# A 256-column first weight slice and six idle matmuls in the opening of a fused attention and 4-bit feed-forward kernel

## The chip, the cores and the metric

The kernel runs on one core of a Trainium2 chip. A core has five engines that run side by side, each with its own instruction stream: TensorE (PE in the profile, its weight loads PEld), VectorE (DVE), ScalarE (ACT), GpSimd (POOL) and SyncE (SP), which here only issues transfers. They meet at semaphores. The metric is device time of one execution in microseconds (us), lower is better. The profile is of one execution of its own.

## The reference

Everything is float32, with x and ctx of shape (32, 64, 512). The core of what is computed:

```python
x = x + xattn(layernorm(x), ctx, ctx, Wq, bq, Wk, bk, Wv, bv, Wo, bo)
x = x + ffn(layernorm(x), gate_w, gate_z, gate_s, up_w, up_z, up_s, down_w, down_z, down_s)

# xattn: 8 heads of 64 columns; W* are 64x64 and act on the axis of length 64
q, k, v = (einsum('oi,bil->bol', W, x) + b[:, None] for each of the three)
p = softmax(q_h @ k_h.T / sqrt(64))
out = einsum('oi,bil->bol', Wo, heads(p @ v_h)) + bo[:, None]

# ffn: integers 0..15, a zero and a scale for each group of 128 rows and each column
W = (w - repeat(z, 128, axis=0)) * repeat(s, 128, axis=0)
out = (silu(x @ W_gate) * (x @ W_up)) @ W_down       # 512 -> 1792 -> 512
```

## The kernel before

**Tiling.** Two batch entries make a *pair* of 128 rows, so there are 16 pairs; four pairs make a *block* of 512 token columns, and there are four blocks. The attention of block 0 has nothing to hide behind. The attention of blocks 1 to 3 is spread over the rounds of the feed-forward (FFN) of the block before it.

**The opening.** The string `START` (L741) is an order written out by hand. Each word such as `2.turn` is a method of `Attention` for one pair: `stats` and `scale` and `apply` (layer norm; `scale` is the power on POOL, L381, and `apply` L112), `k`, `q`, `scores`, `v`, `turn` (softmax weights times Wo, L497), `weigh` (L513), `residual` (L525, which also stores the new x, L528), then `stats2`, `scale2`, `apply2` for the second layer norm, `flip` (transposes on PE, L536) and `high` and `low` (L546 on ACT and L550 on DVE). The last two split the transposed activations into two halves, `hTh` and `hTl`, whose sum is the float32 value. `x_out` words finish a step on ACT or DVE. The opening runs under `tc.manual_schedule()`, so each engine gets its instructions exactly in this order. After it a scheduler orders each engine's stream.

**Weights.** The 4-bit integers come from DRAM as int32 into `ng`, `nu` (gate and up, four row groups `g` of 128 rows, 1792 columns) and `nd` (down, 14 groups of rows). They are loaded by POOL's DMA queue (`load_wide`, `load_down`) in the column slices of the list `wide`: 512, 512, 512, 256 columns. Then the zero point is subtracted in place: POOL does it for each (group, gate or up) piece of a slice (L302), DVE for each row of `nd` (L308). One such subtraction is one step of the generator `weight_steps`; the word `integers` in `START` takes one step. The zero points have first been cast and written to DRAM (`zeros_to_dram`, the word `zeros`), and `load_zeros` reads them back broadcast to 128 partitions, on SP's queue, into `z16` (bfloat16, for gate and up) and `z8` (for down). The pool `zeros` has one buffer of each, so the next slice's zeros are loaded when the last piece of the slice before has been computed.

**The FFN loop.** `gate_up(t, f)` (L595) works on 128 of the 1792 hidden columns: for each of four row groups it does two matmuls of `pg` and two of `pu` (L604), and ACT scales the sum between groups (L614). The last group ends in the Silu (L617), the product `h` on DVE (L620), and its split into `hh` and `hl` on POOL (L630, L631). Two lanes, even and odd f, run two rounds apart; `down(t, f)` (L636) follows six rounds behind. A round (L864) advances the lanes, the attention of the next block, the downs, and `weights`. In round 0, 5 and 13 `load_weights` issues the loads of slices 1, 2 and 3. The first matmul at L604 needs `hTh` of all four pairs, and its PSUM bank is one that the opening's transposes used, so the last `low` must have read it.

**Waiting for products.** `behind_products` makes the first instruction after it wait for the last PE instruction written so far, so that a transfer starts no earlier than that.

Of the kernel before, what the change touches and what calls it, by code (L numbers as in the profile page):

```python
# [26 lines left out]
def kernel(  # L27
# [41 lines left out]
    nc = tc.nc  # L69
# [44 lines left out]
    with ExitStack() as fast:  # L114
# [17 lines left out]

        PARTS = ("c", "xn", "k_eT", "q_e", "v")

        def places(pool):
# [25 lines left out]
        bqk = bias[:, : 2 * D].rearrange("p (m d) -> p m d", m=2)  # L163
        bvo = bias[:, 2 * D :]
        CW = 512
        wide = [(c, min(CW, I - c)) for c in range(0, I, CW)]
        w_T = const.tile([P, 4, D], F32, tag="w_T", name="w_T")
        WK, WV, WQ, WO = range(4)

# [95 lines left out]
        def load_wide(w: bass.AP, src: bass.AP, at: int, n: int):  # L265

            newest["POOL"] = nc.gpsimd.dma_start(w[:, :, at : at + n], src[:, :, at : at + n]).ins

        def load_down(at: int, n: int):
            fs = slice(at // P, (at + n) // P)  # L270
            newest["POOL"] = nc.gpsimd.dma_start(nd[:, fs, :], down_rows[:, fs, :]).ins

        def load_weights(at: int, n: int):

            load_wide(ng, gate_rows, at, n)
            load_wide(nu, up_rows, at, n)
            load_down(at, n)

        def load_zeros(at: int, n: int):
            z16 = zeros.tile([P, 2, KT, CW], BF16, tag="z16", name=f"z16_{at}")  # L280
            z8 = zeros.tile([P, KT, CW], U8, tag="z8", name=f"z8_{at}")
            for m in range(2):
                nc.sync.dma_start(
                    z16[:, m, :, :n], z_rows[m, :, at : at + n].partition_broadcast(P)
                )
            nf = n // P
            zd = z8_dram[at // P * L : (at // P + nf) * L]
            nc.sync.dma_start(
                z8[:, :nf, :].rearrange("p f l -> p (f l)"), zd.partition_broadcast(P)
            )  # L290
            return z16, z8

        def weight_steps(zs):

            for i, (at, n) in enumerate(wide):
                if i:
                    zs = load_zeros(at, n)
                z16, z8 = zs
                for g in range(KT):
                    for m, dst in enumerate((ng, nu)):  # L300
                        piece = dst[:, g, at : at + n]
                        nc.gpsimd.tensor_tensor(  # L302
                            piece, piece.bitcast(F32), z16[:, m, g, :n], ALU.subtract
                        )
                        yield
                for i in range(n // P):
                    piece = nd[:, at // P + i, :]
                    nc.vector.tensor_tensor(piece, piece.bitcast(F32), z8[:, i, :], ALU.subtract)  # L308
                    yield
# [19 lines left out]
        class Attention:  # L329
# [201 lines left out]
            def flip(self):  # L531
                two = self.tile("ph")[:, : self.n, :]
                self.ph = two.rearrange("p i (c d) -> p c i d", d=P)
                for i in range(self.n):
                    for c in range(KT):
                        nc.tensor.transpose(  # L536
                            self.ph[:, c, i, :], self.at["xn"][:, i, ts(c, P)], ident
                        )

            def columns(self, h: dict):  # L540
                t, i = divmod(self.p, PB)
                cols = h[t][:, :, i * P : (i + self.n) * P]
                return cols.rearrange("p c (i d) -> p c i d", d=P)
# [190 lines left out]
        def chain(*gens):  # L734
# [6 lines left out]
        START = """  # L741
            0.stats 0.scale 0.apply 1.stats projections 1.scale biases
            projections_out 1.apply 2.stats 0.k biases_out 2.scale 3.stats 0.q 1.q
            0.k_out 3.scale 0.q_out 1.k gate zeros 1.q_out 0.scores 1.k_out 2.k
            3.apply 1.scores broadcast 0.highest 2.apply 2.k_out 0.less 0.v
            1.highest 0.exp 2.q 1.less 0.v_out 3.q 0.sums 1.exp 2.v 2.q_out 0.divide
            3.k up 2.v_out 1.sums 2.scores 3.q_out 1.divide 3.k_out 1.v 2.highest
            3.scores 1.v_out 2.less 1.turn 3.highest 2.exp 0.turn rows 3.less
            1.turn_out 2.sums 3.exp 1.weigh 0.turn_out 3.sums 2.divide 3.v
            1.residual 1.stats2 3.divide 0.weigh 3.v_out 2.turn 0.residual 0.stats2  # L750
            1.scale2 3.turn down 2.turn_out 2.weigh 3.turn_out 1.apply2 0.scale2
            scales 2.residual 2.stats2 3.weigh scales_out 1.flip 3.residual 3.stats2
            2.scale2 1.high 0.apply2 3.scale2 integers integers integers integers
            2.apply2 0.flip 1.low 2.flip 3.apply2 0.high quotients 3.flip 2.high
            0.low 3.high 2.low 3.low
        """
        place = places(att)
        with (
            tc.tile_pool(name="early", bufs=1) as early,
            tc.tile_pool(name="att0", bufs=1) as att0,  # L760
            tc.tile_pool(name="ps0", bufs=4, space=bass.MemoryType.PSUM) as ps0,
            tc.manual_schedule(),
        ):
            w_nat, b_nat = projection_loads()
# [12 lines left out]
            def first_banks(name: str):  # L777
                return ps0.tile([P, 2, CW], F32, tag="s", name=name)

            @contextmanager  # L780
            def behind_products():

                traced = nc.cur_bb.bb.instructions
                last = next(i for i in reversed(traced) if i.engine == mybir.EngineType.PE)
                n = len(traced)
                yield
                first = traced[n]
                tc.add_manual_dep(  # L790
                    first,
                    last.name,
                    mybir.DependencyInfo(
                        mybir.DependencyClass.Sync, mybir.DependencyReason.DATA
                    ),
                    reason="behind products",
                )

            pairs = [Attention(p, 1, at_first[p // SET], first_banks) for p in range(PB)]
            halves = {}  # L800
            for step in START.split():
                if step[0].isdigit():
                    getattr(pairs[int(step[0])], step[2:])()
                elif step == "gate":
                    load_wide(ng, gate_rows, *wide[0])
                elif step == "zeros":
                    zeros_to_dram()
                elif step == "broadcast":
                    with behind_products():
                        weights = weight_steps(load_zeros(*wide[0]))  # L810
                elif step == "up":
                    with behind_products():
                        load_wide(nu, up_rows, *wide[0])
                elif step == "rows":
                    with behind_products():
                        load_rows(PB // SET)
                elif step == "down":
                    with behind_products():
                        load_down(*wide[0])
                elif step == "integers":  # L820
                    next(weights)
                elif step == "quotients":
                    quotients()
                elif step.endswith("_out"):
                    next(halves[step[:-4]], None)
                else:
                    halves[step] = {
                        "projections": lambda: projections(w_nat),
                        "biases": lambda: biases(b_nat),
                        "scales": lambda: scales(s_nat),  # L830
                    }[step]()
                    next(halves[step])
# [30 lines left out]
        with ExitStack():  # L863
            for r in range(NBLK * ROUNDS + LAG):  # L864
# [16 lines left out]
                with ExitStack() as behind:  # L881
                    for ins in newest.values():
                        behind.enter_context(tc.issue_after(ins))
                    if r in (0, 5, 13):
                        load_weights(*wide[(0, 5, 13).index(r) + 1])
                    if r < ROUNDS:
                        advance(weights, 2 if r < 4 else 1 + r % 2)
                    else:
                        advance(tops, 1 + (r % 4 == 3))
                    if k in FINISH_AT or k + 2 in FINISH_AT:  # L890
                        advance(finishing)
# [120 lines left out]
```

## Time and profile before

| | |
|---|---|
| median of three runs | 457.89 us (454.89 to 458.46) |
| the profiled execution's own time | 457.63 us |
| its span in the profile | 455.3 us |
| busy: PE, PEld, DVE, ACT, POOL | 413.0, 315.3, 330.5, 309.3, 280.4 us |
| matmuls of the FFN, L604 gate and up, mean | 398 to 407 ns, 224 of each of four kinds |
| gate and up integers, L302, mean | 1060 and 1072 ns, 16 of each |
| loads of 1 MB, issue to landing (gate, up, down) | 5.9, 7.9 and 9.6 us |

The span is the time from the first to the last instruction that the profile shows; the 2.3 us between it and the execution's own time lie around it. A busy PE isn't PE at its peak, since the ends of matmuls are modelled. Busy shares are averages: the opening, up to the first L604 at 43.85 us, has another limit than the loop.

### The profile page before, as it was taken

The numbers are of one execution on the slowest core, as the hardware profiler recorded it, in microseconds if no ns is written. First come the engines' busy times: TensorE is split into PE (matmuls) and PEld (weight loads), VectorE is DVE, ScalarE is ACT, GpSimd is POOL, SyncE is SP. The second block draws the span as 40 slices with busy tenths as digits, with TensorE's granted clock in tenths as the row PEclk, the third lists the DMA queues.
The fourth block names the chain that finished last, engine by engine and source line by source line (L and its number), as shares of the span: only waits on it lengthen the run. The fifth ranks groups of instructions, "written<-read, shape, count | busy, mean of one in ns | idle before, by whom it ended". The sixth has DMA issues, their size and how long they took to land.

```text
span 455.3 us, 10322 instructions
## 1 busy us (share of the span) xinstructions
PE 413.0 (91%) x4175; PEld 315.3 (69%) x4175; DVE 330.5 (73%) x510; ACT 309.3 (68%) x473; POOL 280.4 (62%) x293
## 2 busy tenths in 40 slices
PE   4854998998999999999999899999999999999991
PEld 4642564766677776777778577786778888887870
DVE  5959553797979983696869775586869655668672
ACT  2332489665787669686788569785688788777750
POOL 5335749658474487676787676664566887883311
PEclk9988799999999999999999999999999999999996
DMA  6677959436102020141000012130001012100004
GB/s 205 204 246 229 254 188 273 118 100 183 53 26 74 2 93 1 45 141 50 1 23 25 2 48 94 48 94 1 1 1 48 1 47 94 46 1 0 1 2 145
DMA packets 20928, 36.55 MB, mean 80 GB/s; under 512 B 1848, under 2 KB 7432, under 8 KB 20872
## 3 DMA queue, kind: packets, MB, share of 16 engines
q1 hardware_dynamic: 14056, 24.20, 16.2%
q0 software_dynamic: 6208, 11.01, 8.8%
q8 instruction: 35, 0.57, 0.5%
q10 hardware_dynamic: 608, 0.59, 0.4%
q14 instruction: 21, 0.17, 0.1%
HBM read 27.37 MB, written 8.42 MB: 79 GB/s over the span
## 4 chain that ended last, share of the span: by engine, by line
PE 45%; POOL 23%; issue 15%; DVE 10%; ACT 4%; DMA 1%; ACTq 0%; POOLq 0%; DVEq 0%
PE pg L604 11%; PE pu L604 11%; PE pd L649 6%; POOL hl L631 6%; PE pd L652 5%; POOL squares L325 4%; POOL squares L323 4%; POOL hh L630 3%; DVE xn_set L112 2%; DVE y L660 2%; POOL nu L302 2%; POOL q_e_set L488 1%; POOL ng L302 1%; DVE k_eT_set L411 1%; DMA w_nat<-in_L_xattn_Wo_dram 1%
## 5 line engine op out<-in xcount | busy, mean ns | idle before, releaser
L660 DVE SCALAR_TENSOR_TENSOR y<-pd,s_all,y 128x512 f32<-128x512 f32 x204 | 150.1, 743 | 47.6 <-PE pd L652 45.1
L614 ACT ACTIVATE pg<-pg,s_q 128x512 f32<-128x512 f32 x168 | 111.5, 665 | 76.4 <-PE pg L604 75.0
L614 ACT ACTIVATE pu<-pu,s_q 128x512 f32<-128x512 f32 x168 | 110.7, 659 | 4.5 <-PE pu L604 4.4
L604 PE MATMUL pg<-hTh,ng 128*128 128x512 f32 x224 | 91.3, 407 | 6.3 <-POOL nu L302 2.9
L649 PE MATMUL pd<-hh,nd 128*128 128x512 f32 x224 | 93.9, 419 | 1.6 <-DVE y L660 1.1
L630 POOL CAST hh<-h 128x512 fp32r<-128x512 f32 x55 | 35.0, 636 | 93.0 <-DVE h L620 91.2
L604 PE MATMUL pu<-hTh,nu 128*128 128x512 f32 x224 | 90.6, 404 | 0.9 <-POOL nu L302 0.5
L604 PE MATMUL pu<-hTl,nu 128*128 128x512 f32 x224 | 89.3, 399 | 0.0
L604 PE MATMUL pg<-hTl,ng 128*128 128x512 f32 x224 | 89.2, 398 | 0.0
L652 PE MATMUL pd<-hl,nd 128*128 128x512 f32 x224 | 88.7, 397 | 0.0
L631 POOL TENSOR_TENSOR hl<-h,hh 128x512 fp32r<-128x512 f32 x55 | 72.0, 1310 | 4.4
L620 DVE SCALAR_TENSOR_TENSOR h<-pu,s_all,g 128x512 f32<-128x512 f32 x56 | 41.8, 746 | 34.2 <-ACT g L617 27.8
L325 POOL TENSOR_TENSOR squares<-squares 128x512 f32<-128x512 f32 (+1 forms) x46 | 55.1, 1197 | 1.7
L604 PEld LDWEIGHTS pg<-hTh,ng 128*128 128x128 f32 x224 | 42.2, 188 | 20.1 <-ACT pg L614 4.2
L649 PEld LDWEIGHTS pd<-hh,nd 128*128 128x128 f32 x224 | 42.0, 188 | 18.0 <-DVE y L660 4.9
L604 PEld LDWEIGHTS pu<-hTh,nu 128*128 128x128 f32 x224 | 42.3, 189 | 14.0 <-ACT pu L614 2.7
L604 PEld LDWEIGHTS pu<-hTl,nu 128*128 128x128 f32 x224 | 42.3, 189 | 9.7 <-issue 0.4
L604 PEld LDWEIGHTS pg<-hTl,ng 128*128 128x128 f32 x224 | 42.4, 189 | 9.1
L617 ACT ACTIVATE g<-pg,s_all 128x512 f32<-128x512 f32 x56 | 38.7, 692 | 13.9 <-PE pg L604 12.2
L652 PEld LDWEIGHTS pd<-hl,nd 128*128 128x128 f32 x224 | 42.2, 188 | 7.4
L302 POOL TENSOR_TENSOR ng<-ng,z 128x512 fp32r<-128x512 f32 (+1 forms) x16 | 17.0, 1060 | 8.1 <-DMA z<-z_dram 8.1
L302 POOL TENSOR_TENSOR nu<-nu,z 128x512 fp32r<-128x512 f32 (+1 forms) x16 | 17.2, 1072 | 0.0
(290 smaller groups left out, 480.0 us busy)
## 6 DMA issues: line engine op xcount, KB each, us to landing
ng<-in_L_ffn_gate_w_dram POOLq DMA_DIRECT2D x3, 1024.0 KB, 5.9
z<-z_dram SPq DMA_DIRECT2D x6, 512.0 KB
nu<-in_L_ffn_up_w_dram POOLq DMA_DIRECT2D x3, 1024.0 KB, 7.9
c_set<-in_ctx_dram SPq DMA_DIRECT2D x6, 512.0 KB
x<-in_x_dram SPq DMA_DIRECT2D x6, 512.0 KB
nd<-in_L_ffn_down_w_dram POOLq DMA_DIRECT2D x3, 1024.0 KB, 9.6
x_dram<-x SPq DMA_DIRECT2D x6, 512.0 KB
r<-x_dram SPq DMA_DIRECT2D x6, 512.0 KB
```

Source lines behind the costliest of these rows:

```text
L302: nc.gpsimd.tensor_tensor(piece, piece.bitcast(F32), z16[:, m, g, :n], ALU.subtract)
L323: nc.gpsimd.tensor_tensor(square[:, :n], piece, piece, ALU.mult)
L325: nc.gpsimd.tensor_tensor(total[:, :n], total[:, :n], square[:, :n], ALU.add)
L604: nc.tensor.matmul(acc, w[:, g, ts(f, P)], half[:, g, :], start=(g == 0 and half is hi), stop=(g == KT - 1 and half is lo), skip_group_che ...
L614: nc.scalar.activation(acc, acc, AF.Copy, scale=by)
L617: nc.scalar.activation(g_sb, acc, AF.Silu, scale=by)
L620: ins = nc.vector.scalar_tensor_tensor(h_sb, acc, by, g_sb, ALU.mult, ALU.mult)
L630: nc.gpsimd.tensor_copy(hh, h_sb)
L631: ins = nc.gpsimd.tensor_tensor(hl, h_sb, hh.bitcast(F32), ALU.subtract)
L649: nc.tensor.matmul(pd, w, h_hi[t, f], start=(t, f) != LAST, stop=False, skip_group_check=True)
L652: nc.tensor.matmul(pd, w, h_lo[t, f], start=False, stop=True, skip_group_check=True)
L660: ins = nc.vector.scalar_tensor_tensor(y, pd, by, y, ALU.mult, ALU.add)
```

## The change

The first slice of gate and up gets 256 columns in place of 512: `wide` is now 256, 512, 512, 512. All eight gate and up pieces of that slice are made within the opening (eight words `integers` where there were four). The loads move within `START`: `gate` and `up` (now 512 KB each) go later, `down` goes, and `more_gate`, `more` and `more_up` load slice 1 in the opening, with the down rows of slices 0 and 1 in one transfer of 1.5 MB. The zeros of slice 0 get a buffer of their own in the pool `early`, and `z8` is loaded apart, when the generator comes to the slice. The loop's loads of round 0 go; rounds 5 and 13 load slices 2 and 3. A new step `warm` does two matmuls of 256 columns into a PSUM tile that nobody reads; it stands three times in `START`.

```diff
+        WARM = 2
...
-        wide = [(c, min(CW, I - c)) for c in range(0, I, CW)]
+        FIRST = 256
+        wide = [(0, FIRST)] + [(c, CW) for c in range(FIRST, I, CW)]
...
-        def load_zeros(at: int, n: int):
-            z16 = zeros.tile([P, 2, KT, CW], BF16, tag="z16", name=f"z16_{at}")
-            z8 = zeros.tile([P, KT, CW], U8, tag="z8", name=f"z8_{at}")
+        def load_zeros(at: int, n: int, pool=zeros):
+            z16 = pool.tile([P, 2, KT, n], BF16, tag="z16", name=f"z16_{at}")
             for m in range(2):
...
+        def load_down_zeros(at: int, n: int):
+            z8 = zeros.tile([P, KT, CW], U8, tag="z8", name=f"z8_{at}")[:, : n // P, :]
...
+        def weight_steps():
+            for at, n in wide:
+                z16 = early_zeros.pop(0) if early_zeros else load_zeros(at, n)
+                z8 = load_down_zeros(at, n)
+                pieces = [(m, g) for g in range(KT) for m in range(2)]
+                for m, g in pieces if at else sorted(pieces):
+                    piece = (ng, nu)[m][:, g, at : at + n]
+                    nc.gpsimd.tensor_tensor(
+                        piece, piece.bitcast(F32), z16[:, m, g, :], ALU.subtract
+                    )
+                    yield
...
+            def warm(self):
+                idle = self.tile("idle")
+                for _ in range(WARM):
+                    nc.tensor.matmul(
+                        idle[:, 0, : 2 * P], ident, self.x[:, 0, : 2 * P], start=True, stop=True
+                    )
...
         START = """
...
-            0.k_out 3.scale 0.q_out 1.k gate zeros 1.q_out 0.scores 1.k_out 2.k
-            3.apply 1.scores broadcast 0.highest 2.apply 2.k_out 0.less 0.v
-            1.highest 0.exp 2.q 1.less 0.v_out 3.q 0.sums 1.exp 2.v 2.q_out 0.divide
-            3.k up 2.v_out 1.sums 2.scores 3.q_out 1.divide 3.k_out 1.v 2.highest
-            3.scores 1.v_out 2.less 1.turn 3.highest 2.exp 0.turn rows 3.less
-            1.turn_out 2.sums 3.exp 1.weigh 0.turn_out 3.sums 2.divide 3.v
-            1.residual 1.stats2 3.divide 0.weigh 3.v_out 2.turn 0.residual 0.stats2
-            1.scale2 3.turn down 2.turn_out 2.weigh 3.turn_out 1.apply2 0.scale2
-            scales 2.residual 2.stats2 3.weigh scales_out 1.flip 3.residual 3.stats2
-            2.scale2 1.high 0.apply2 3.scale2 integers integers integers integers
-            2.apply2 0.flip 1.low 2.flip 3.apply2 0.high quotients 3.flip 2.high
-            0.low 3.high 2.low 3.low
+            0.k_out 3.scale 0.q_out 1.k zeros 1.q_out 0.scores 1.k_out 2.k 3.apply
+            1.scores broadcast 0.highest 2.apply 2.k_out 0.less 0.v 1.highest 0.exp
+            2.q 1.less 0.v_out 3.q 0.sums 1.exp 2.v 2.q_out 0.divide 3.k gate
+            2.v_out 1.sums 2.scores 3.q_out 1.divide 3.k_out 1.v 2.highest 3.scores
+            1.v_out 2.less 1.turn 3.highest 2.exp 0.turn up rows 3.less 1.turn_out
+            2.sums 3.exp 1.weigh 0.turn_out 3.sums 2.divide 3.v 1.residual 1.stats2
+            3.divide integers integers integers integers 0.weigh 3.v_out 2.turn
+            0.residual 0.stats2 1.scale2 more_gate integers 3.turn more 2.turn_out
+            2.weigh 3.turn_out 1.apply2 0.scale2 integers integers scales 2.residual
+            2.stats2 3.weigh 2.warm scales_out 1.flip 3.warm 3.residual 3.stats2
+            2.scale2 integers 1.high 0.apply2 3.scale2 more_up 2.apply2 0.flip 1.low
+            2.flip 3.apply2 0.high quotients 3.flip 3.warm 2.high 0.low 3.high 2.low
+            3.low
         """
...
-                        weights = weight_steps(load_zeros(*wide[0]))
+                        early_zeros.append(load_zeros(*wide[0], early))
+                elif step == "gate":
+                    with behind_products():
+                        load_wide(ng, gate_rows, *wide[0])
...
-                elif step == "down":
+                elif step == "more":
                     with behind_products():
-                        load_down(*wide[0])
+                        early_zeros.append(load_zeros(*wide[1]))
+                elif step == "more_gate":
+                    load_wide(ng, gate_rows, *wide[1])
+                elif step == "more_up":
+                    load_wide(nu, up_rows, *wide[1])
+                    load_down(0, wide[1][0] + wide[1][1])
...
-                    if r in (0, 5, 13):
-                        load_weights(*wide[(0, 5, 13).index(r) + 1])
+                    if r in (5, 13):
+                        load_weights(*wide[(5, 13).index(r) + 2])
```

More of the change, by code (lines that the diff above doesn't have):

```diff
@@ L277, in load_weights @@
             load_down(at, n)
-        def load_zeros(at: int, n: int):
-            z16 = zeros.tile([P, 2, KT, CW], BF16, tag="z16", name=f"z16_{at}")
-            z8 = zeros.tile([P, KT, CW], U8, tag="z8", name=f"z8_{at}")
+        def load_zeros(at: int, n: int, pool=zeros):
+            z16 = pool.tile([P, 2, KT, n], BF16, tag="z16", name=f"z16_{at}")
             for m in range(2):
[L283 to L305, printed above, removed]
+                nc.sync.dma_start(z16[:, m], z_rows[m, :, at : at + n].partition_broadcast(P))
+            return z16
+        def load_down_zeros(at: int, n: int):
+            z8 = zeros.tile([P, KT, CW], U8, tag="z8", name=f"z8_{at}")[:, : n // P, :]
+            zd = z8_dram[at // P * L : (at + n) // P * L]
+            nc.sync.dma_start(z8.rearrange("p f l -> p (f l)"), zd.partition_broadcast(P))
+            return z8
+        def weight_steps():
[9 more added lines that the diff above has]
+                    yield
                 for i in range(n // P):
@@ L778, in first_banks @@
                 return ps0.tile([P, 2, CW], F32, tag="s", name=name)
+            early_zeros, weights = [], weight_steps()
             @contextmanager
@@ L803 @@
                     getattr(pairs[int(step[0])], step[2:])()
-                elif step == "gate":
-                    load_wide(ng, gate_rows, *wide[0])
                 elif step == "zeros":
```

## The prediction

> **What bounds the kernel now.** I read the forty slices of the page first, then the waits, then the timeline of the opening and the stretches after it.
>
> ```profile
> PE   4854998998999999999999899999999999999991
> PEclk9988799999999999999999999999999999999996
> DMA  6677959436102020141000012130001012100004
> ```
>
> From about 110 us on PE is busy nine tenths or more: that part is bound by PE, and this change barely touches it. The first four slices (45 us) are half empty, and the next few have dents. What can be won lies there. Two stalls make it.
>
> ```profile
> 22.10 0.57 PE L497 MATMUL pe<-w_T,q_e_set 64*64 64x64 f32 x23 [0.16 <-PE pe L497]
> 27.82 0.50 PE L497 MATMUL pe<-w_T,q_e_set 64*64 64x64 f32 x9 [5.15 <-issue]
> ...
> 29.24 0.88 DVE L525 SCALAR_TENSOR_TENSOR x<-po,bias,x 128x256 f32<-128x256 f32 x2 [4.34 <-PE po L513]
> ...
> 41.87 1.87 DVE L550 TENSOR_TENSOR hTl<-ph,hTh 128x512 fp32r<-128x512 f32 x3
> ...
> 43.85 0.47 PE L604 MATMUL pg<-hTh,ng 128*128 128x512 f32 x1 [2.89 <-POOL nu L302]
> ```
>
> In the timeline PE stops for 5.15 us in the middle of one step (`0.turn`), whose matmuls all have the same inputs: no semaphore can hold it there. DVE then waits 4.34 us for PE, and from 29.24 to 43.74 us it works almost without a gap; PE's first L604 starts 0.1 us after DVE's last `low`. The page names POOL for that wait, but POOL's piece had ended at 42.97. So the opening ends with DVE's chain of 14.5 us, and what started that chain late is PE's stop.
>
> I read the stop as an instruction fetch. PE and PEld show 984 instructions up to 22.7 us; with some forty that aren't shown, that is 1024.
>
> ```profile
> q8 instruction: 35, 0.57, 0.5%
> ```
>
> In the table of queues q8 moves 16.3 KB a packet. Cut into short stretches, the trace has its packets near 11.7, 16.3, 25.3, 28.9 and 32.3 us, and the 256th, 512th, 768th and 1024th PE instruction falls near 10.7, 14.4, 18.7 and 22.7: a packet each time one block has been used up. The third is 6.5 us late where the others are 1 to 2. At 18.7 us 1.25 MB of zeros had just been issued (17.24 to 18.74) and 1 MB of `nu` followed at 19.23; the transfer engines moved 378 GB/s from 24.1 to 27.5.
>
> ```profile
> 44.50:47.90 3.40, 3.40 (x20) 1.85 (x19) 3.12 (x9) 1.99 (x3) 1.42 (x2) 0.50 0.02 5
> 47.90:51.30 3.40, 3.40 (x55) 2.44 (x55) 1.99 (x4) 0.66 (x1) 3.40 (x5) 0.50 0.79 192
> ```
>
> These are stretches of 3.4 us: length, busy time of PE, PEld, DVE, ACT and POOL with counts, granted PE clock, DMA share, GB/s. The FFN starts at half clock, for 6.8 us. And in the table of waits:
>
> ```profile
> POOL ng L302 <- DMA z<-z_dram: 8.1, 1, 8.1
> ```
>
> POOL stands until 62.8 us for the zeros of slice 1, since their buffer comes free only with the last piece of slice 0.
>
> **What the Trainium skill says.** "Runtime: NRT & Kernel Launch", Instruction fetch mechanics: instructions come in 16 KiB blocks of 256, fetched by a DMA queue of the sequencer's own, mostly hidden. The trace agrees on the block (16.3 KB) and has one that isn't hidden. "TensorE: Matmul & The Clock Gate", Part 1: the array falls to half clock after an idle window of about 3.4 us, with windows that run free of the kernel. The trace agrees in length (half clock 37.7 to 41.1 and 44.5 to 51.3), but here a window that was busy for 0.65 of 3.4 us was enough to lose the clock. "SBUF — State Buffer", Who interferes with whom: VectorE operations with two SBUF inputs or in a two-port mode contend with GpSimd. L112 takes 0.54 us alone and 0.84 beside L302 at 38.9 us, which agrees.
>
> **The change part by part**, against the profiled execution (457.63 us, near the median of 457.89).
>
> *Loads before 23 us.* The gate load no longer stands before the zero casts (0.81 us of POOL) nor runs beside their write, for whose landing SP waited 4.1 us. The zeros of slice 0 halve to 512 KB and can start some 2 us earlier, at about 15. At 18.7 us, when the block is asked for, the queues are then almost empty; gate (512 KB) is issued at about 19.3, after `0.divide`, and `up` only after `0.turn`. So the block comes in the 1 to 2 us of its neighbours, before PE needs it at 22.7. DVE can take `1.residual` when its own sums end, at 24.9 in place of 29.24: **-4.3 us**. The next block (asked for at 22.7, wanted near 26.7) shares the engines with 1.5 MB of c, `up` and x rows, some 4 us at 380 GB/s: 0 to 1 us; I take 0.
>
> *New work and waits in DVE's chain.* Eight pieces of 256 columns (0.67 us each, the shortest L302) are 5.4 us of POOL for 4.6 before. The first four stand ahead of `1.scale2`: POOL has `2.divide` and `3.divide` until 26.3, the pieces until 29.0, so `1.scale2` ends at 29.6. DVE reaches `1.apply2` near 28.9: 0.7 to 0.8 us lost. The fifth waits for `up`, with `0.scale2` behind it; issued at 23 and landing by 30, it leaves `0.scale2` ready near 31.6, and DVE has 3.9 us of other pairs' residuals first (two of 0.88 with statistics of 1.05): nothing, as long as `up` is there by 34. Longer contention with POOL: 0.3. On PE the second `warm` must read x before `3.residual` may write it, and itself stands behind `1.flip` and the first `warm`, which waits for `2.residual`. A matmul of 256 columns takes 0.15 to 0.27 us (32 of L434 in their groups), four with a flip some 1.2 us, against 1.05 of `2.stats2`: 0.1 to 0.3. Together **+1.3**. The first L604 comes near 40.8: opening **-3.0** in all, 0 to -4.3.
>
> *SP and POOL queues.* SP now has `z8` and the 1 MB of slice 1's zeros between the x stores, ahead of the 6th and 7th pairs' rows; a store that waits for a residual holds them up by less than a DVE step. POOL issues more_gate, more_up and the 1.5 MB of down (0.8 us each) ahead of `rs_4to`, where it issued three in round 0 behind it: even.
>
> *FFN from 43.85 to 76 us (32.2 us).* PE is idle for 3.9 us of it (8.20-8.10, 8.00-6.75, 8.00-7.67, 8.00-5.75), and half clock costs at most 3.4 more; ACT needs 23.1 us and POOL 21.2. What goes: the 8.1 us stand of POOL, as slice 1's zeros come early; the four pieces of slice 0 that PE met at 49.6 to 54.1; part of the half clock. The last `warm` leaves PE idle for some 2.5 us in place of 2.9, so I count half. What is late next: the ping-pong with ACT (ACT waits 9.0 us for `pg` here), and the down rows. Of 7.3 us I take **-4.6**; nothing is won at the one end, 7.3 at the other.
>
> *Down rows.* They are last in a queue of about 7 MB after 28.5 us, so at 380 GB/s they land near 47, at 250 near 56. On DVE their first two subtractions stand ahead of `q_e` of pairs 4 and 5 and of the first `h`; PE's scores wait for `q_e`. PE has about 12 us of work first, to 53. Up to 50 it costs nothing, then a us for each.
>
> *Removed or moved at no cost:* the six matmuls otherwise (PE idles there), the last slice of 512 for 256 (same total of columns, L302 takes 28 us for 29 in the loop).
>
> Sum: 457.63 - 3.0 - 4.6 = **450.0**. The loop after 76 us is PE-bound, so what is won before should reach the end.
>
> **The rivals.** *The fetch still stops PE* (25%). It could be late for another reason than the traffic, as the queue's own latency; for it: it's only one of seven fetches that was late, against: that one met the full queues. Then `up`, behind `0.turn`, is issued at 28.4 with `2.divide` and `3.divide` behind it, `1.scale2` ends at 34.5, and the opening ends 1.2 us later than before: 457.6 + 1.2 - 4.6 = 454.2.
> *The opening gains, the FFN doesn't* (10%): slice 2 is wanted in round 12, was wanted in round 16, and its zeros again wait for slice 1's last piece; the 8.1 us stand returns near 60 us and eats the 4.6: 454 to 455.
> *The down rows are late* (14%), the case on the other side. At 380 GB/s they don't matter; from a landing at 56 the FFN's gain is gone, and from about 63 the kernel is over 1% slower, as `q_e`, `h` and all of POOL behind `hh` wait. At 65: 457.6 - 3.0 + 9 = 463.6. Against it: 7 MB would have to crawl at under 200 GB/s, and the 44 to 64 us stretch moved 238 on average with empty times in it.
> *No effect* (3%): the DMA traffic moves with the work: 457.
>
> **How the numbers follow.** The likeliest case (48%) is 450.0, with 445.5 to 453. A measurement of this kernel tells about 1% (4.6 us) from no change, so the line is at 453.1. Faster: the 48, most of the FFN-only cases below the line, some of the rest, 0.66. Slower: 0.14. Within: 0.20. The range runs from 445.0 to 457.0: at the lower end both stalls go whole (457.6-4.3-7.3=446) with a little more, at the upper the rivals that gain half.
>
> **What would show it.** No idle PE over 2 us between 20 and 28 us; DVE's `1.residual` at 25; the first L604 at 40 to 41.5; a POOL wait on zeros under 3 us; half clock after the first L604 for 3.4 us or less. I'd be wrong if the stop stays near 22.7, if a fetch packet is late elsewhere, or if DVE stands at L308 (then named for the down rows) past 53.

## The result, and the profile after

The median went from 458.15 us (12 runs, 454.89 to 459.22) to **455.63 us** (12 runs, 453.12 to 457.22). The ratio is 0.9958, with a 95% interval of 0.9936 to 0.9979. So it is 1.9 us faster by the ratio and 2.5 by the two medians, where 7.6 were forecast. The profiled execution took 454.78 us, its span 452.9.

The page of the kernel after, tenths busy in forty slices (11.3 us each):

```profile
PE   4867889979989999999999899999999999999991
PEclk9988999999999999999999999999999999999997
DMA  6399629178011110231010002220001012100004
```

The second to seventh digits of PE stand at 867889 where they were 854998, so the opening has become fuller. But there is a 7 in the ninth slice and an 8 in the twelfth (90 to 102 and 124 to 136 us), in the part of the loop where PE was said to be the bound.

In after.py the lines below the new code are 9 higher: L604, L617 and L660 are now L613, L626 and L669. `warm` is L545, `low` L559. In the timeline of the opening (start, length, engine, line, operation, count, idle time before it and its releaser):

```profile
24.68 0.82 DVE L525 SCALAR_TENSOR_TENSOR x<-po,bias,x 128x256 f32<-128x256 f32 x2
...
29.26 0.98 DVE L112 TENSOR_SCALAR xn_set<-x,mv,rs 128x512 f32<-128x512 f32 x1 [0.69 <-POOL rs L381]
...
35.07 0.88 DVE L525 SCALAR_TENSOR_TENSOR x<-po,bias,x 128x256 f32<-128x256 f32 x2 [2.92 <-PE idle L545]
```

```profile
31.16 2.04 PE L545 MATMUL idle<-x,ident 128*128 128x256 f32 x4 [2.65 <-DVE x L525]
33.00 1.06 PE L536 MATMUL ph<-ident,xn_set 128*128 128x128 f32 x4
33.86 1.17 PE L545 MATMUL idle<-x,ident 128*128 128x256 f32 x4
...
42.25 0.47 PE L613 MATMUL pg<-hTh,ng 128*128 128x512 f32 x1 [0.60 <-DVE hTl L559]
```

`1.residual` starts at 24.68 in place of 29.24: PE's stop is gone. The fourth pair's residual then stands 2.92 us for idle matmuls that read its x. The chain on PE is the one that the prediction named (first `warm`, flip, second `warm`), but it takes 3.9 us; the granted clock was 0.51 from 30.8 to 34.2 us. The FFN starts at 42.25 us, 1.60 earlier than before. From 41.1 us on the clock is full (before: half from 44.5 to 51.3).

Two waits are new. They are the two longest of PE after 50 us:

```profile
96.85 0.50 PE L658 MATMUL pd<-hh,nd 128*128 128x512 f32 x1 [2.40 <-DVE y L669]
```

```profile
130.72 0.50 PE L613 MATMUL pu<-hTh,nu 128*128 128x512 f32 x1 [2.05 <-POOL nu L302]
```

What they do is seen by following one instruction through the loop: the start of the Silu of hidden tile f of block 0, read from ACT's timeline (L617 before, L626 after). A block has f from 0 to 13.

| f | before | after | after less before |
|---|---|---|---|
| 0 | 60.54 | 53.48 | -7.06 |
| 3 | 78.65 | 73.00 | -5.65 |
| 6 | 100.67 | 94.48 | -6.19 |
| 7 | 112.92 | 109.79 | -3.13 |
| 10 | 132.25 | 128.82 | -3.43 |
| 11 | 140.54 | 139.07 | -1.47 |
| 0 of block 1 | 160.78 | 158.31 | -2.47 |
| 6 of block 3 | 398.13 | 395.94 | -2.19 |

Some 6 to 7 us were won by 60 us and still held at 94. Then 3.1 us are given back between the Silus of f 6 and 7, and 2.0 between those of 10 and 11: the places of the two waits. (The rest of the wandering is attention work that stands at other places between them.) After that the lead stays to the end.

### The profile page after: what moved, and what is told of

Same layout as the page of the kernel before. It is cut to its first block, busy times and chain, and to the rows that moved or that the text cites. A ratio compares the mean times of both kernels' runs of the same rounds, so it can differ in the third digit from the quotient of the medians.

```text
span 452.9 us, 10346 instructions
## 1 busy us (share of the span) xinstructions
PE 413.7 (91%) x4187; PEld 316.3 (70%) x4187; DVE 327.6 (72%) x510; ACT 309.1 (68%) x473; POOL 280.5 (62%) x292
## 4 chain that ended last, share of the span: by engine, by line
PE 46%; POOL 22%; DVE 14%; issue 12%; ACT 3%; DMA 2%; POOLq 0%; ACTq 0%; DVEq 0%
PE pu L613 12%; PE pg L613 12%; PE pd L658 7%; POOL hl L640 6%; PE pd L661 6%; POOL squares L325 4%; POOL squares L323 4%; POOL hh L639 3%; DVE xn_set L112 3%; DVE y L669 3%; DVE k_eT_set L411 2%; POOL ng L302 1%; POOL q_e_set L488 1%; POOL nu L302 1%; DMA x<-in_x_dram 1%
## 5 line engine op out<-in xcount | busy, mean ns | idle before, releaser
L669 DVE SCALAR_TENSOR_TENSOR y<-pd,s_all,y 128x512 f32<-128x512 f32 x204 | 150.3, 744 | 52.8 <-PE pd L661 50.9
L613 PE MATMUL pg<-hTh,ng 128*128 128x512 f32 x224 | 90.1, 402 | 3.4 <-ACT g L626 1.7
L613 PE MATMUL pu<-hTh,nu 128*128 128x512 f32 x224 | 90.6, 405 | 2.6 <-POOL nu L302 2.0
L613 PE MATMUL pu<-hTl,nu 128*128 128x512 f32 x224 | 88.8, 397 | 0.0
L613 PE MATMUL pg<-hTl,ng 128*128 128x512 f32 x224 | 88.6, 396 | 0.0
L613 PEld LDWEIGHTS pg<-hTh,ng 128*128 128x128 f32 x224 | 42.0, 188 | 16.6 <-issue 2.9
L613 PEld LDWEIGHTS pu<-hTh,nu 128*128 128x128 f32 x224 | 42.0, 188 | 15.2 <-POOL nu L302 2.5
L613 PEld LDWEIGHTS pu<-hTl,nu 128*128 128x128 f32 x224 | 42.1, 188 | 9.4 <-issue 0.4
L613 PEld LDWEIGHTS pg<-hTl,ng 128*128 128x128 f32 x224 | 42.1, 188 | 9.4
L626 ACT ACTIVATE g<-pg,s_all 128x512 f32<-128x512 f32 x56 | 38.7, 691 | 13.7 <-PE pg L613 12.1
L302 POOL TENSOR_TENSOR ng<-ng,z 128x512 fp32r<-128x512 f32 (+1 forms) x16 | 16.7, 1048 | 3.3 <-DMA z<-z_dram 3.3
L302 POOL TENSOR_TENSOR nu<-nu,z 128x512 fp32r<-128x512 f32 (+1 forms) x16 | 16.8, 1056 | 0.0
```

The source lines that it names most:

```text
L302: nc.gpsimd.tensor_tensor(piece, piece.bitcast(F32), z16[:, m, g, :], ALU.subtract)
L613: nc.tensor.matmul(acc, w[:, g, ts(f, P)], half[:, g, :], start=(g == 0 and half is hi), stop=(g == KT - 1 and half is lo), skip_group_che ...
L626: nc.scalar.activation(g_sb, acc, AF.Silu, scale=by)
L669: ins = nc.vector.scalar_tensor_tensor(y, pd, by, y, ALU.mult, ALU.add)
```

## Experiments

Ratios are to runs of the kernel before on the same chip. The kernels ran in three groups (e1 to e4, e5 to e8, e9 to e12), in which the median of the kernel before was 457.1, 457.23 and 456.88 us. Four kernels first tested the opening and the zeros.

**The idle matmuls read another pair (e1).** The first of the two `3.warm` becomes `2.warm`.

```diff
-            2.stats2 3.weigh 2.warm scales_out 1.flip 3.warm 3.residual 3.stats2
+            2.stats2 3.weigh 2.warm scales_out 1.flip 2.warm 3.residual 3.stats2
```

> The changed kernel with one word altered: the second idle step reads x of pair 2 (already final) in place of pair 3, so the residual of pair 3 no longer waits for idle matmuls. Theory 1 (that wait of 2.9 us is on the path and its worth is carried to the end): no DVE wait on L545, first FFN matmul near 39.4 us in place of 42.25, kernel about 2.5 us faster than the changed one, near 453, ratio to before about 0.990. Theory 2 (the lead is lost later to DVE and POOL between 90 and 140 us whatever its size): first FFN matmul just as early, but the end unmoved, 455 to 456, ratio 0.995. If the clock falls at the new place: in between, with half clock after 39.4 in the profile.

Measured: 458.34 us, ratio 1.0026 (1.0004 to 1.0048). The fourth pair's residual no longer waits (32.35 us in place of 35.07) and the FFN starts at 39.86, 2.4 us before the changed kernel. But the end is slower, which neither theory had. DVE's timeline and then PE's, of e1:

```profile
39.52 1.27 DVE L375 BATCH_NORM_STATS2 st_4to<-x 128x6 f32<-128x512 f32 x2
40.71 0.16 DVE L376 BATCH_NORM_AGGREGATE mv_4to<-st_4to 128x2 f32<-128x6 f32 x1
43.61 0.70 DVE L375 BATCH_NORM_STATS2 st_6to<-x 128x6 f32<-128x512 f32 x1 [2.73 <-DMA x<-in_x_dram]
```

```profile
45.38 0.39 PE L613 MATMUL pu<-hTh,nu 128*128 128x512 f32 x1
49.78 1.09 PE L434 MATMUL pv_4to<-c_set,w_T 64*64 64x256 f32 x16 [4.01 <-DVE k_eT_set L411]
```

Here is a wait that the changed kernel doesn't have. The statistics of pair 6 (counted from 0) need its x rows, which land at 43.6 us; in the changed kernel DVE came to that step at 43.18 and did not wait. In DVE's order the end of the statistics of pairs 4 and 5, their `rs`, L112 and `k_eT` all stand behind it, and PE behind them. The queues moved 400 GB/s from 41.1 to 44.5. A faster opening only comes sooner to this landing. PE's idle time then took the clock: 0.53 from 51.3 to 54.7, and again half near 100 and 134 us, after the two waits of the loop. That is one execution. Over all runs the mean granted clock has a median of 0.979 in e1 and 0.985 in the changed kernel, and the changed kernel's own runs get some 2.1 us longer for each 0.01 of clock. By that estimate the clock accounts for about 1.3 of the 2.7 us between the two medians; the rest isn't explained.

**No idle matmuls (e2), and only the last pair of them (e3).** In e2 all three `warm` words go; in e3 only the last stays.

```diff
-            2.stats2 3.weigh 2.warm scales_out 1.flip 3.warm 3.residual 3.stats2
+            2.stats2 3.weigh scales_out 1.flip 3.residual 3.stats2
...
-            2.flip 3.apply2 0.high quotients 3.flip 3.warm 2.high 0.low 3.high 2.low
+            2.flip 3.apply2 0.high quotients 3.flip 2.high 0.low 3.high 2.low
```

> The changed kernel without any of the six idle matmuls. Theory 1 (they cost 2.9 us of the opening and keep the clock for the FFN): first FFN matmul near 39 us, then half clock for 3.4 to 6.8 us, so the first Silu comes about as late as in the changed kernel (53.5 us) and the end is within 1 us of it, 455 to 456.5. Theory 2 (they keep nothing, the FFN's gain is from the integers made early): full clock or no matter, first Silu near 50.5, end near 453. Theory 3 (they are worth more than they cost): end at 457 or more.

> Only the last two idle matmuls are left, between the last transposes and the first FFN matmul. If those alone keep the clock: first FFN matmul near 39, full clock after it, end near 452.5 to 453. If the clock needs all three places: half clock after 39, end like the kernel with none.

Measured: e2 457.79 us, ratio 1.0017 (0.9991 to 1.0042), as theory 3 had it; e3 457.12, ratio 1.0005 (0.9975 to 1.0034). In e2 the FFN starts at 39.59 us, at half clock up to 44.2, and the first Silu comes at 54.81 (53.48 in the changed kernel). In e3 it starts at 39.91, the clock is 0.93 from 40.8 to 44.2 and full after it, and the first Silu comes at 52.91; the end is not the 452.5 to 453 that was expected of it. In e2 PE stands 2.5 us and DVE 3.7 us for the same k_eT and x; in e3 2.3 and 1.7. Without all six matmuls what the change had won is gone, so in the changed kernel they are worth some 2 to 3 us; for e3 the interval just meets that of the changed kernel.

**The zeros of slice 3 on POOL's queue (e4).** In the changed kernel POOL stands 3.3 us near 110 us for zeros of slice 3, whose transfer SP issues late.

```diff
...
+                if at == 768:
+                    early_zeros.append(load_zeros(*wide[3], queue=nc.gpsimd))
                 for i in range(n // P):
```

(The lines left out let `load_zeros` take a queue.)

> The changed kernel, but the gate and up zeros of the last slice are loaded by POOL's queue right after the last piece of the slice before, in place of SP's queue, where they stood behind the down zeros (which wait for DVE) and the next ctx rows (which wait for PE) and were issued 5.6 us late. Theory 1 (that order on SP is what POOL waits for at 110.7 us and PE at 128.7): POOL's wait of 3.3 us and PE's of 2.0 us on L302 go, end 1.5 to 2 us earlier, near 454. Theory 2 (POOL is simply full there, with 512-column pieces where there were 256): PE's wait on L302 stays over 1 us and the end within 0.7 us of the changed kernel.

Measured: 455.46 us, ratio 0.9963 (0.9943 to 0.9983): as without the edit. POOL's wait for zeros fell from 3.3 to 1.3 us, and PE's wait for `nu` stayed at 2.04. So the zeros weren't what PE waited for. POOL's timeline of the changed kernel shows what was:

```profile
123.98 1.16 POOL L302 TENSOR_TENSOR ng<-ng,z 128x512 fp32r<-128x512 f32 x1
126.64 1.00 POOL L639 CAST hh<-h 128x512 fp32r<-128x512 f32 x1 [1.50 <-DVE h L629]
127.72 1.84 POOL L640 TENSOR_TENSOR hl<-h,hh 128x512 fp32r<-128x512 f32 x1
129.52 1.15 POOL L302 TENSOR_TENSOR nu<-nu,z 128x512 fp32r<-128x512 f32 x1
```

The last piece of slice 3 stands in POOL's order behind `hh` and `hl` of f = 9, and these behind DVE's `h`. PE wants the piece at 128.7. The kernel before had the same order at its last slice, two f later, and almost got through. Its PE:

```profile
146.13 0.50 PE L604 MATMUL pu<-hTh,nu 128*128 128x512 f32 x1 [0.54 <-POOL nu L302]
```

There the two Silus around this point (f = 11 and 12) lie 5.09 us apart, since attention work stands between them; between those of f = 9 and 10 it is 3.78. So in the changed kernel PE comes 1.3 us sooner, and the piece takes 1.15 us in place of 0.67.

Counting the steps shows how both places can follow from the new cut at the old **pace**. The generator gives two weight steps in each of rounds 0 to 3, then one and two by turns. Counted so, the last piece of slice 3 is step 42, taken in round 21 for PE's round 23; before it was step 44, in round 25 for round 27. The margin in rounds is the same two, but all of it lies four rounds (two f) earlier, among other work. Slice 2's down rows are now steps 31 to 34, in rounds 13 to 15; before, no down row fell into rounds 12 to 15. DVE's timeline of the changed kernel in them:

```profile
91.85 0.68 DVE L308 TENSOR_TENSOR nd<-nd,z 128x512 fp32r<-128x512 f32 x1
92.45 0.74 DVE L669 SCALAR_TENSOR_TENSOR y<-pd,s_all,y 128x512 f32<-128x512 f32 x1
93.11 3.03 DVE L112 TENSOR_SCALAR xn_set<-x,mv_6to,rs_6to 128x512 f32<-128x512 f32 x2
96.06 0.73 DVE L669 SCALAR_TENSOR_TENSOR y<-pd,s_all,y 128x512 f32<-128x512 f32 x1
```

PE's wait until 96.85 is for the `y` at 96.06. It stands behind one of the four down rows (91.85) and behind the two L112, and beside these POOL has `hl` and three issues of loads (93.08 to 96.6).

**Two steps earlier (e5), and no subtraction for slice 2's down rows (e6).** The second leaves the four subtractions out and is only there for its trace.

```diff
-                        advance(weights, 2 if r < 4 else 1 + r % 2)
+                        advance(weights, 2 if r < 7 else 1 + r % 2)
```

> In the first block's rounds 4 and 6 two weight steps are taken in place of one, so that from round 6 on every piece of slices 2 and 3 stands two steps earlier in POOL's and DVE's order. Theory A (what was won is given back because the new cut makes slice 3 fall due two rounds earlier while the pace of the steps stayed, so that the last piece of nu stands behind hh and hl of the f before it): PE's wait of 2.05 us for POOL nu near 128.7 us goes, the lead on the kernel before is still about 3 us or more at the eleventh and twelfth Silu (after: 1.47 and 1.25), and the median comes 1.5 to 3 us below the changed kernel's: 453 to 454, ratio 0.988 to 0.992. If the subtractions of the down rows in DVE's full rounds matter too, PE's wait of 2.40 us near 94.5 shrinks as well, for one of them leaves those rounds. Theory B (the loop has no slack to give: DVE and ACT take the time elsewhere): the wait for POOL goes but another wait of about the same length comes within 10 us; ratio 0.995 to 0.998, as with the changed kernel.

("Two rounds earlier" there should read two f, four rounds.)

```diff
-                    nc.vector.tensor_tensor(piece, piece.bitcast(F32), z8[:, i, :], ALU.subtract)
+                    if at != 768:
+                        nc.vector.tensor_tensor(piece, piece.bitcast(F32), z8[:, i, :], ALU.subtract)
                     yield
```

> This leaves out the four subtractions of zeros from the down rows of slice 2 (the rows from 768 to 1280); the step itself stays, so that nothing else moves. Theory A (these four, 0.66 us each, fall into the rounds in which DVE is busy 8.00 of 8 us, and PE's wait of 2.40 us for DVE's y near 94.5 us is theirs): without them DVE is free for about 2 us between 91 and 102 us, PE's wait for y falls to under 1 us, and the lead at the eighth Silu is 4.5 to 6 us in place of 3.1. Theory B (the wait is that of the two L112, which take 3.03 us beside POOL): the wait stays at 2 us or more, and the lead at the eighth Silu stays at 3 to 3.5.

Measured, e5: **446.18 us** (445.34 to 447.69), ratio 0.9762 (0.9734 to 0.9791), far more than was expected. Its lead on before is 8.40 us at f = 6, 9.85 at f = 7, 9.93 at f = 11 and 11.22 in the last tiles of block 3. Both waits are gone; the longest of PE between 50 and 150 us is 1.27 us, for ACT. The stretches of the changed kernel, then of e5 (length, busy time of PE, PEld, DVE, ACT and POOL, granted clock, DMA share, GB/s):

```profile
92.00:110.00 18.00, 14.73 (x186) 10.00 (x185) 14.32 (x18) 9.31 (x14) 7.63 (x8) 1.00 1.01 303
110.00:130.00 20.00, 18.52 (x193) 13.66 (x192) 15.01 (x21) 16.45 (x24) 16.84 (x15) 1.00 0.02 5
130.00:150.00 20.00, 19.28 (x145) 15.56 (x146) 17.37 (x31) 13.39 (x22) 7.11 (x8) 1.00 0.16 53
```

```profile
92.00:110.00 18.00, 18.00 (x266) 13.64 (x265) 14.62 (x20) 10.64 (x17) 12.48 (x14) 1.00 0.75 227
110.00:130.00 20.00, 19.48 (x199) 14.49 (x198) 17.93 (x29) 17.25 (x26) 11.11 (x11) 1.00 0.07 28
130.00:150.00 20.00, 20.00 (x173) 15.35 (x174) 17.57 (x34) 15.12 (x23) 10.25 (x13) 1.00 0.18 61
```

PE is busy 57.48 of these 58 us in place of 52.53: 4.95 us of the 9.0 by which the two executions differ in block 3. Another 1.4 us is less idle time between 42 and 76 us; 0.7 us of lead is there at the first Silu already, though the opening has the same code. Over the whole span PE is idle for 32.7 us in place of 39.2. The other 2.9 us between the spans is the same 4187 matmul records counting as busy for less time, and isn't explained further. Nor did the line move the two waits alone: the scheduler, too, ordered DVE otherwise. In e5 the two L112 of pairs 6 and 7 stand behind `k_eT` (L411, at 95.26 us), in the changed kernel ahead of it (100.36). How much of the gain is the earlier steps and how much this order wasn't separated.

Measured, e6: one execution of 454.39 us, span 452.3. PE's wait for `y` near 95 us fell from 2.40 to 0.91 us and the lead at f = 7 rose from 3.13 to 5.06, near what theory A had. The wait for the last `nu` piece is still there (1.7 us), and 3.2 us are lost at it, so the end is where it was. The two L112 still took 1.96 us in e6. In e5 nothing of POOL ran beside them:

```profile
97.04 0.99 DVE L112 TENSOR_SCALAR xn_set<-x,mv_6to,rs_6to 128x512 f32<-128x512 f32 x2
```

So the first wait has two parts: the down row ahead of the L112, and what POOL does beside these. The two aren't independent, for without the row the L112 came earlier beside POOL's work (3.03 us became 1.96). The transfers are not what made L112 long: the queues moved 362 GB/s beside the 0.99 us of e5 and 58 GB/s beside the 3.03 us.

**The down rows split (e7).** As e1, with the down rows of slice 1 asked for a round later.

```diff
-                    load_down(0, wide[1][0] + wide[1][1])
+                    load_down(*wide[0])
...
+                    if r == 1:
+                        load_down(*wide[1])
                     if r in (5, 13):
```

> As e1 (the idle matmuls read the third pair's x, so they hold up no residual), and the down rows of slice 1 (1 MB) are asked for a round later, apart from those of slice 0. Theory A (in e1 the freed 2.3 us were lost since DVE then stood 2.73 us for the x rows of the last pairs, which come with some 7 MB in the queues, and PE behind it 4.0 us for k_eT): with 1 MB less ahead, x lands 1 to 2.5 us earlier, the wait for x falls under 1.5 us and PE's wait for k_eT under 2.5; the lead at the first Silu grows from 6.6 to 8 or more, and the down rows of slice 0 hold nothing. The end gains less than that, for the later waits near 95 and 129 us are still there: 454 to 457. Theory B (the x rows are late for SP's order, not for the traffic): x lands at 43.5 us as in e1, and nothing changes against e1: 458.

Measured: 463.17 us, ratio 1.0137 (1.0105 to 1.017), a miss for both theories. The x rows land 0.8 us earlier (42.8), but PE's wait for `k_eT` is 10.5 us:

```profile
46.74 0.69 DVE L308 TENSOR_TENSOR nd<-nd,z 128x512 fp32r<-128x512 f32 x1 [3.14 <-DMA nd<-in_L_ffn_down_w_dram]
47.35 0.16 DVE L377 TENSOR_SCALAR rs_4to<-mv_4to 128x2 f32<-128x2 f32 x1
47.42 0.68 DVE L308 TENSOR_TENSOR nd<-nd,z 128x512 fp32r<-128x512 f32 x1
48.72 5.95 DVE L112 TENSOR_SCALAR xn_set<-x,mv_4to,rs_4to 128x512 f32<-128x512 f32 x2 [0.61 <-POOL rs_4to L381]
```

In this kernel the scheduler put the first down row ahead of the end of the statistics, so these now stood for its landing. And two L112 took 5.95 us, one of them 5.50, while POOL issued a load and made four pieces in a row (49.45 to 53.93). That the traffic holds the x rows is neither shown nor excluded by this run, since what DVE did behind them changed too.

**The zeros of slice 1 early (e8).** The word `more` moves up to stand behind `broadcast`, which puts 1 MB into the queues just when PE's fourth block of instructions is asked for.

```diff
-            1.scores broadcast 0.highest 2.apply 2.k_out 0.less 0.v 1.highest 0.exp
+            1.scores broadcast more 0.highest 2.apply 2.k_out 0.less 0.v 1.highest 0.exp
...
-            0.residual 0.stats2 1.scale2 more_gate integers 3.turn more 2.turn_out
+            0.residual 0.stats2 1.scale2 more_gate integers 3.turn 2.turn_out
```

> The 1 MB of zeros of slice 1 is asked for right behind that of slice 0, near 16 us, so that the queues are full when PE's fourth block of instructions is fetched, as they were before the change. Theory A (the fetch was late for the traffic): the packet of the instruction queue that comes at 19 us in the changed kernel comes at 22 to 26, PE stops for 2 us or more near 22.7 in the middle of the step with the 64x64 transposes, with no release shown, and DVE's residual of pair 1 starts at 26.5 to 29 in place of 24.7. Theory B (it was late because of the gate load or the write of the zeros to DRAM, or by chance): the packet comes at about 19 to 20 and the residual at 24.7 to 25.2.

Measured: one execution of 455.71 us. PE's timeline of e8:

```profile
23.16 0.57 PE L497 MATMUL pe<-w_T,q_e_set 64*64 64x64 f32 x23 [0.16 <-PE pe L497]
25.55 0.35 PE L497 MATMUL pe<-w_T,q_e_set 64*64 64x64 f32 x9 [1.81 <-issue]
```

The stop is back, at the same matmul of the same step, 23 before it and 9 after. The packet of the instruction queue lies between 22.5 and 23 us; in the changed kernel it lies between 19 and 20, and there is no stop. The residual of pair 1 starts at 26.43. It is a smaller stop (1.81 for 5.15 us), a little under what theory A gave. Of the other traces e9, which has the old opening, has the stop as well (4.87 us), and none with the changed opening has it. So 1 MB of zeros moved to an earlier place was enough to make the fetch late, in one execution. In it the FFN starts at 43.28 us, 1.0 later than in the changed kernel, and the end is no later.

**Is it the pace alone? (e9), and with the right pace: no idle matmuls (e10), idle matmuls of another pair (e11), two more steps (e12).** e9 has the one line of e5 in the kernel before; e10 and e11 are e5 with the edits of e2 and e1; e12 takes two steps in rounds 8 and 10 as well.

> The kernel before, and of all edits only the pace: in rounds 4 and 6 two weight steps in place of one. Theory A (the change's own parts and the pace belong together: the kernel before had its last slice two rounds later, its pieces of 256 columns and no wait for POOL between 90 and 150 us, so the pace has nothing to free there): the median stays within 1% of before, ratio 0.99 to 1.005. Theory B (the pace alone is worth what e5 gained, because two DVE steps leave the full rounds in this kernel as well): ratio 0.975 to 0.985, and the change itself is worth nothing.

> As e5 without the six idle matmuls. Theory A (they pay: the FFN's first 3.4 us or more are otherwise at half clock, 1.7 us or more): 1 to 3 us above e5, 447 to 449. Theory B (they cost DVE as much, 2.92 us before the residual of pair 3, as they save on the clock, and the FFN's start is bound by the transfers until 48 us): within 1 us of e5. Rival C (without them DVE's chain is free by 2 us and nothing of it is lost now that the loop has slack): 1 to 2 us below e5, 444 to 445.

> As e5, and the idle matmuls read the third pair's x, so that they hold up no residual. Theory A (the opening's rest, some 2.3 us, is lost to the x rows of the last pairs, which land at 43.5 us whatever DVE does): DVE stands 2 to 3 us for x near 41 us, PE 3 to 4 us for k_eT near 46, and the median is within 1.5 us of e5, above it rather than below. Theory B (the loss seen in e1 came from the wait for DVE and POOL later): 2 us below e5, 444.

> As e5 with two more steps taken early (in rounds 8 and 10). Theory A (one round of slack was what was missing, and two steps give it): within 1 us of e5; POOL's waits for DMA grow, since the weights of slice 2 are asked for in round 5 and are wanted sooner. Theory B (each step earlier helps DVE's full rounds further): 1 to 3 us below e5.

| | pace as it was | two steps earlier |
|---|---|---|
| kernel before | 1 | 0.9952 (0.9935 to 0.9969) |
| with the change | 0.9958 (0.9936 to 0.9979) | 0.9762 (0.9734 to 0.9791) |
| the change, no idle matmuls | 1.0017 (0.9991 to 1.0042) | 0.9798 (0.9765 to 0.9832) |
| the change, idle matmuls of the third pair | 1.0026 (1.0004 to 1.0048) | 0.9785 (0.9744 to 0.9827) |
| the change, four steps earlier | | 0.9815 (0.9777 to 0.9853) |

The pace alone is worth 2.2 us to the kernel before, the change alone 1.9, both 10.9. So the change is worth about 8.7 us where the loop can keep it, more than four times as much by the middle values. Theory A of e9 held for the time, but not in that there was nothing to free. A stretch of the kernel before, then of e9:

```profile
92.00:110.00 18.00, 15.78 (x140) 11.55 (x139) 16.80 (x24) 11.40 (x18) 13.11 (x14) 1.00 0.55 158
92.00:110.00 18.00, 17.11 (x206) 12.91 (x205) 14.43 (x20) 12.05 (x18) 14.54 (x15) 1.00 0.56 154
```

From 92 to 150 us PE is busy 56.45 us in e9 and 54.48 before, 1.97 us more, so here the kernel before had idle time of PE that an earlier order of the weight steps took away. In e11 DVE stands 2.3 us for x and PE 3.6 for `k_eT`, as in e1, and the end is no better than e5: with either pace the opening then meets the landing of the x rows. Whether the idle matmuls pay is clear with the old pace and not with the new one, where the intervals overlap. Four steps earlier gain nothing more than two: POOL's longest wait for weights is then 5.0 us, for the gate rows of slice 3. e5 is faster than both kernels of the comparison, and it is the version to keep.

## Why the prediction was wrong

It forecast 450.0 and faster by over 1%; it came to 455.63, faster by 0.4%. Its steps one by one:

- **PE's stop is an instruction fetch behind the traffic, -4.3: right.** `1.residual` came 4.56 us earlier; the packets lie near 11, 15, 19, 24 and 28 us; e8 brought a smaller stop back by moving 1 MB of traffic alone.
- **New work and waits in DVE's chain, +1.3: mis-sized.** `1.scale2` cost 0.69 as worked out. The `warm` wait was put at 0.1 to 0.3 us with matmuls at 0.15 to 0.27, and measured 2.92: two `warm` steps and a flip took the 3.9 us seen above where 1.2 were put, most of it at half clock, which the sum left out. So the opening gained 1.6 in place of 3.0. But e1 and e11 show that this term doesn't explain the end: with the wait gone, the x rows' landing takes its place.
- **FFN up to 76 us, -4.6: right.** The lead grew from 1.6 at the start to 7.06 at the first Silu, and was 5.65 at f = 3: 4.1 to 5.5 us from the FFN. With the opening, 5.7 to 6.2 of the 7.6 us were there between 73 and 94 us. POOL's stand of 8.1 us and the half clock behind 41.1 us are gone.
- **Down rows landing at 47 to 56, no cost up to some 50: right.** They landed at 51.5 us and DVE stood 2.27 us for them; no wait of PE for them is seen.
- **"The loop after 76 us is PE-bound, so what is won before should reach the end": this step failed.** It took the loop for bound by PE from a row whose tenths stand at nine throughout only from about 110 us. Between 92 and 110 us PE was busy 15.78 of 18 us in the kernel before and is busy 14.73 after; and e9, with nothing but another pace, takes 2.2 us off the kernel before. Of a lead of 6.2 us at f = 6, 3.1 went at the wait for DVE near 95 us and 2.0 at the wait for POOL near 129, in the very part that the change was said barely to touch. The prediction counted the L302 pieces and found the same number of columns; it didn't ask beside what work each weight step now falls, and beside what its product is wanted. It did so for slice 2's zeros alone, in the second rival.
- **The rivals.** The fetch did not stop PE. "The opening gains, the FFN doesn't" gave 454 to 455, near what came, but by another cause at another place: no stand for zeros returned near 60 us. The one on the other side, late down rows, did not come. The range of 445.0 to 457.0 held the time, since the rivals that gain half reached there. That was luck: what took the other half is in none of them.

## What to carry to other kernels

A lead won in one stage reaches the end only if every later stage has slack for it: follow one repeated instruction through both traces, and the place where the lead shrinks names the next limit. When a change moves the boundaries of a staged load, list again for each stage the round in which it is produced and the round in which it is wanted; counted in rounds the margin may be the same and in time too short. Here one line of pace made the same change worth 8.7 us in place of 1.9. And a wait taken away from a chain is worth only the distance to the next landing that the chain meets.

## What the runs showed of the hardware

- Two L112 (128x512, float32) take 0.99 us with nothing on POOL beside them (e5), 2.68 beside L302 pieces (the changed kernel, 45.47 us), and 5.95 beside four pieces in a row (e7). The Trainium skill's "SBUF — State Buffer", Who interferes with whom, calls the port pair that VectorE and GpSimd share an exclusive lock; the traces fit that, for the pieces of POOL kept their 1.14 to 1.16 us in e7 while one L112 took 5.50. The prediction had 0.3 us for such contention in all.
- The fetch of PE instructions that lies at 19 to 20 us in the changed kernel came about 3 us later with 1 MB more in the queues (e8) and 6 us later in the kernel before; it stopped PE for 1.81 and 5.15 us.
- Two idle matmuls of 128x256 float32 (four records) took 2.04 us in the changed kernel's first `warm`, at 31.16 us, and 1.17 in its second, at 33.86. The granted clock was 0.51 from 30.8 to 34.2 us and 0.98 from 34.3 to 37.7.
- Waits of 2.40 and 2.05 us in the loop sometimes also took the clock: in e1's profile it is half for some 3.4 us after each, in the changed kernel's after neither.
